# The first tokens' projections with their features in two quarters and one half, in a fused transformer block on one Trainium2 core

## The chip, the cores and the metric

The kernel runs on one core of a Trainium2 chip. The metric is the device time of one execution in microseconds (us). Each run's time is listed; a profile is one further execution with the hardware profiler on. Engines are named as in the profile: PE (TensorE matmul), PEld (its weight load), DVE (VectorE), ACT (ScalarE), POOL (GpSimd), SP (SyncE, which here issues nearly all DMA transfers).

## What is computed

One adaptive-layernorm transformer block over 2048 tokens of 1024 features, in float32. A vector c gives six modulation vectors, two of which (`sa`, `ca`) shift and scale the normalized input of the attention:

```python
mod = (_silu(L0_c) @ L0_wmod).reshape(L0_c.shape[0], 6, 1, -1)
sa, ca, ga, sb, cb, gb = (mod[:, 0], mod[:, 1], mod[:, 2], mod[:, 3], mod[:, 4], mod[:, 5])
...
h = _layernorm(x, axis=-1) * (1 + ca) + sa
x = x + ga * _L0_attn_ref(h, L0_attn_Wq, L0_attn_Wk, L0_attn_Wv, L0_attn_Wo)
h = _layernorm(x, axis=-1) * (1 + cb) + sb
x = x + gb * _L0_ffn_ref(h, L0_ffn_route_w, L0_ffn_A, L0_ffn_Bw)
```

The attention has 32 query heads and 8 key and value heads of 32 features, rotary positions and a causal mask. The feed-forward part routes each token to one of 8 low-rank experts. What matters here is the very first stage: `q = h @ Wq`, `k = h @ Wk`, `v = h @ Wv` for the first 256 tokens, where h needs `ca` and `sa`.

## The kernel before

The features (1024) lie in 8 chunks of 128 on the partitions. `h_t` holds h transposed: [128, 8 chunks, 256 tokens].

**Modulation** (L846 to L907). `Modulation(i, half)` makes 512 of the 1024 features of modulation vector i. It has two parts. The first, `mr` (L874), multiplies the matrix wmod, which comes in four w tiles of [128, 2, 512] (256 rows and 512 columns each, 512 KB), by the vector silu(c), and copies the result to `rows` on DVE (L880). The second, `mc` (L886), turns the rows into columns, one per chunk, and writes them to `mod_cols[i]` on DVE (L892 or L894). i = 1 is the scale `ca` (plus one), i = 0 the shift `sa`.

**Project** (L940). `Project(b)` handles 256 tokens in two token tiles of 128: `flip` transposes the normalized x on PE into a PSUM bank (L835) and applies scale and shift on the way to `h_t`, on ACT for the first half of the features (L822) and on DVE for the second (L826). Then values and keys (L764, `by_columns`) and queries (L1059) accumulate over the chunks. `keep_values` copies the values on ACT; `keep_keys` and `keep_queries` apply the rotary positions on DVE and POOL (L933 to L938).

**Streams** (L659). `weights` is a queue of loads with a pool of NW = 5 tiles, `tokens` one with NX = 4. `pump` issues the next loads while a buffer is free, `free(n)` gives n buffers back and pumps. Loads are issued in order on SP, and a load into a buffer waits on SP until PE has read the buffer's earlier tile. Eight DMA semaphores are used in turn, so that a load also waits for the one eight places before it.

**The opening** (`open_up`, L1507) is an order written out by hand. `fill(n)` issues the next n parts of the items; the first four items are Modulation (1, half 0), (0, half 0), (1, half 1), (0, half 1). The opening issues both parts of the first two, then the flips of the features 0 to 511 (`kh` = 0), then values, keys and queries over these four chunks, with the third and fourth Modulation between them, then the flips and the projections of the features 512 to 1023. The weights of the first two projections stay resident: `vk` tiles hold four chunks of wv and wk side by side, `wq` tiles two chunks of half of wq's columns. In the middle stand the loads of the second half, of the rotary tables cos and sin (`load_rotation`) and of the next tokens; near the end the norm of the second project's x (`second.pre()`). Six PSUM banks hold the sums of values, keys and four query groups; the two others are used in turn by Modulation and flips.

After the opening a planner (`plan_order`, with estimated costs of each part) sets the order of everything that is left. That order is fixed when the kernel is built.

Of the kernel before, what the change touches and what calls it, by code (L numbers as in the profile page):

```python
# [11 lines left out]
F32 = mybir.dt.float32  # L12
# [6 lines left out]
P = 128  # L19
T = 2048  # L20
D = 1024
# [5 lines left out]
QB = 512  # L27
NQB = T // QB
TB = 256
# [523 lines left out]
def adaln_block_kernel(  # L553
# [24 lines left out]
    nc = tc.nc  # L578
# [15 lines left out]
    ident = const.tile([P, P], F32, name="ident")  # L594
# [64 lines left out]
    class Stream:  # L659
        def __init__(self, pool, tag, depth):  # L660
            self.pool, self.tag, self.depth = pool, tag, depth
            self.loads, self.tiles = [], []
            self.freed = self.used = 0

        def pump(self, most=1 << 30):
            while len(self.tiles) < min(len(self.loads), self.freed + self.depth, most):
                n = len(self.tiles)
                shape, load = self.loads[n]
                t = self.pool.tile(shape, F32, tag=self.tag, name=f"{self.tag}_{n}")
                load(t)  # L670
                self.tiles.append(t)
# [14 lines left out]
    weights = Stream(wpool, "w", NW)  # L686
    tokens = Stream(xpool, "x", NX)

    def want_wmod(i, half):
        for kp in range(NC // 2):  # L690
            col = i * D + half * 512
            src = wmod[kp * 2 * P : (kp + 1) * 2 * P, col : col + 512].rearrange(
                "(k p) n -> p k n", p=P
            )
            weights.loads.append(([P, 2, 512], lambda t, s=src: nc.sync.dma_start(t, s)))

    resident = {}

    def load_values_keys(kh):

        rows = slice(kh * 512, (kh + 1) * 512)
        t = epool.tile([P, 4, QB], F32, tag="et", name=f"vk_{kh}")
        for i, w in enumerate((wv, wk)):
            nc.sync.dma_start(
                t[:, :, i * TB : (i + 1) * TB], w[rows, :].rearrange("(k p) n -> p k n", p=P)
            )
        resident["vk", kh] = t

    def load_queries(kh, half):
        for kp in (2 * kh, 2 * kh + 1):  # L710
            t = qpool.tile([P, 2, QB], F32, tag="q", name=f"wq_{half}_{kp}")
            nc.sync.dma_start(
                t,
                wq[kp * 2 * P : (kp + 1) * 2 * P, half * 512 : (half + 1) * 512].rearrange(
                    "(k p) n -> p k n", p=P
                ),
            )
            resident["q", half, kp] = t

    def want_qkv():  # L720
        for w in (wv, wk):
# [124 lines left out]
    class Modulation:  # L846
# [1 line left out]

        when = -1

        def __init__(self, i, half):
            self.i, self.half = i, half

        def plan(self, push):
            slow = 0.2 if self.i in mod_cols else 2.4
            return [
                Part(1.7, "C", True, (("dve", 0.7),), chunks=4, push=push),
                Part(0.9, "W", True, (("dve", slow),), frees=4),
            ]

        def want(self):
            want_wmod(self.i, self.half)

        def pre(self):
            return []

        def main(self, following):
            i, half = self.i, self.half
            parts = weights.take(4)
            ps = bank(f"mr_{i}_{half}")  # L870
            for r in range(2):
                for q in range(4):
                    k = r * 4 + q
                    nc.tensor.matmul(  # L874
                        ps[q * HD : (q + 1) * HD, :], silu_p[:, k, :], parts[k // 2][:, k % 2, :],
                        start=(r == 0), stop=(r == 1),
                    )
                weights.free(2)
            rows = two.tile([P, 512], F32, tag="half", bufs=3, name=f"rows_{i}_{half}")
            nc.vector.tensor_copy(rows, ps)  # L880
            following()
            yield 1.7, True
            ps = bank(f"mc_{i}_{half}")
            if i in mod_cols:
                for j in range(4):
                    nc.tensor.matmul(  # L886
                        ps[:, j : j + 1], rows[:, j * P : (j + 1) * P], ones_p[:, 0:1],
                        start=True, stop=True,
                    )
                dst = mod_cols[i][:, half * 4 : half * 4 + 4]  # L890
                if i in (1, 4):
                    nc.vector.tensor_scalar_add(dst, ps[:, 0:4], 1.0)  # L892
                else:
                    nc.vector.tensor_copy(dst, ps[:, 0:4])  # L894
            else:


                nc.tensor.matmul(ps, ones_p, rows, start=True, stop=True)
                cols = slice(half * 512, (half + 1) * 512)
                sgn = two.tile([P, 512], F32, tag="half", bufs=3, name=f"gsgn_{i}_{half}")  # L900
# [39 lines left out]
    class Project:  # L940
# [521 lines left out]
    m = {(i, half): Modulation(i, half) for i in (2, 3, 4, 5) for half in range(2)}  # L1462
# [35 lines left out]
    def fill(n=1):  # L1498
        for _ in range(n + 4):
            step = advance()  # L1500
            assert step is not None
            n -= bool(step[0])
            if not n:
                return step[0]
        raise AssertionError("the next part of an item cannot be issued yet")

    def open_up():  # L1507


# [6 lines left out]
        load_values_keys(0)  # L1516
        load_queries(0, 0)
        fill(2)
        opening.start()
        for s in range(2):  # L1520
            opening.flip(s, 0)
        chosen[:0] = range(6)
        banks = [bank("open") for i in range(6)]

        def values(kh):
            for s in range(2):
                for k in range(4 * kh, 4 * kh + 4):
                    opening.value(banks[0], s, k)

        def keys(kh):  # L1530
            for a in range(2):
                for k in range(4 * kh, 4 * kh + 4):
                    opening.key(banks[1], a, k)

        def queries(kh, i):
            for a in range(2):
                for k in range(4 * kh, 4 * kh + 4):
                    opening.query(banks[2 + i], i // 2, 2 * (i % 2) + a, k)

        values(0)  # L1540
        keys(0)
        load_queries(0, 1)
        fill(2)
        load_values_keys(1)
        for half in range(2):
            load_queries(1, half)
        tokens.pump()
        cs = load_rotation(0, 2)
        for i in range(4):
            opening.query_tiles(i // 2, i % 2)  # L1550
        queries(0, 0)
        queries(0, 1)
        fill(2)
        queries(0, 2)
        for s in range(2):
            opening.flip(s, 1)
            tokens.free()
        sign_rotation(cs)
        for _, act in second.pre():
            act()  # L1560
        queries(0, 3)
        values(1)
        keys(1)
        opening.keep_values(banks[0])
        opening.keep_keys(banks[1])
        for half in range(2):
            for hp in range(2):
                queries(1, 2 * half + hp)
            for hp in range(2):
                opening.keep_queries(banks[2 + 2 * half + hp], half, hp)  # L1570
        chosen.clear()
# [357 lines left out]
```

## Time and profile before

| | us |
|---|---|
| time, median of 3 runs | 1755.12 (1754.39 to 1757.01) |
| the profiled execution's own time | 1754.72 |
| its span | 1753.0 |
| mean granted clock of the span | 0.996 |

The first 60 us, in windows of 10 us (busy time of each engine in us; PEclk is the granted clock of PE, 1.00 is full speed):

| from:to us | PE | DVE | ACT | POOL | PEclk | GB/s moved |
|---|---|---|---|---|---|---|
| 0:10 | 1.20 | 1.19 | 2.77 | 8.73 | 1.00 | 263 |
| 10:20 | 8.47 | 5.12 | 3.19 | 0.00 | 0.83 | 361 |
| 20:30 | 9.13 | 0.85 | 2.90 | 0.00 | 1.00 | 384 |
| 30:40 | 9.16 | 0.85 | 0.00 | 0.00 | 1.00 | 366 |
| 40:50 | 9.16 | 2.25 | 0.00 | 0.00 | 1.00 | 386 |
| 50:60 | 10.00 | 6.32 | 4.26 | 0.00 | 1.00 | 372 |

In this stage the transfers run all the time, and PE is the busiest engine from 10 us on. A matmul's busy time is modelled, so that PE can count as busy while it waits a little between two matmuls.

### The profile page before, as it was taken

To read this page: it belongs to the slowest core of one execution; us is meant where nothing else is said; L and a number is where in the kernel's file an instruction comes from. 1 tells how busy PE (TensorE), PEld (TensorE's weight loads), DVE (VectorE), ACT (ScalarE), POOL (GpSimd) and SP (SyncE) were. 2 spreads that over 40 slices of the span, in tenths; PEclk is the share of its full clock that TensorE was granted. 3 is DMA by queue.
4 is the path that set the end of the run, shared out by engine and by line. 5 is a ranking of instruction groups with operands and counts; after the bars stand their busy time and mean duration, and the time that the engine had idled before them with its cause. 6 is when DMAs were issued, how large, how long until landed. Compare 5 with 4: busy or idle time off the path is not lost.

```text
span 1753.0 us, 55172 instructions
## 1 busy us (share of the span) xinstructions
PE 1716.7 (98%) x24616; PEld 700.3 (40%) x24616; DVE 1084.6 (62%) x2140; ACT 740.4 (42%) x1643; POOL 1296.5 (74%) x640
## 2 busy tenths in 40 slices
PE   7999999999999999999999999999999999999998
PEld 3655554444444433334444443323323333333333
DVE  1455556756656764675667545756675675776486
ACT  2203423443543433445435444244444544454463
POOL 1235646478878775869786989789889899898951
PEclk9999999999999999999999999999999999999999
DMA  9502323212322512222013011110111111101001
GB/s 346 193 27 80 115 84 104 63 62 98 104 63 66 180 72 83 73 79 67 24 60 128 26 50 49 68 44 37 50 54 46 48 50 50 73 26 49 34 5 50
DMA packets 69069, 130.52 MB, mean 74 GB/s; under 512 B 3808, under 2 KB 20832, under 8 KB 68832
## 3 DMA queue, kind: packets, MB, share of 16 engines
q1 hardware_dynamic: 67504, 125.85, 20.9%
q8 instruction: 193, 3.16, 0.8%
q10 hardware_dynamic: 1328, 1.15, 0.2%
q14 instruction: 44, 0.36, 0.1%
HBM read 118.59 MB, written 8.39 MB: 72 GB/s over the span
## 4 chain that ended last, share of the span: by engine, by line
PE 77%; POOL 14%; DVE 3%; issue 2%; DMA 1%; ACT 1%; POOLq 0%; SPq 0%; DVEq 0%; ACTq 0%
PE sm L1618 13%; POOL acc L1744 12%; PE po L1726 11%; PE sc L1708 11%; PE pq L1059 11%; PE pw L764 10%; PE sc L1694 4%; PE pk L764 3%; PE pv L764 2%; PE pd L1753 2%; PE open L1059 2%; DVE mx L1625 1%; PE pf L764 1%; PE pa L764 1%; PE sm L1605 1%
## 5 line engine op out<-in xcount | busy, mean ns | idle before, releaser
L1625 DVE TENSOR_REDUCE mx<-sm 128x1 f32<-128x512 f32 (+3 forms) x1280 | 687.4, 604 | 400.1 <-PE sm L1618 399.2
L1744 POOL TENSOR_TENSOR acc<-acc,et 128x2048 f32<-128x2048 f32 (+1 forms) x242 | 905.0, 3739 | 27.6 <-ACT et L1716 14.2
L1716 ACT ACTIVATE et<-sc 128x512 f32<-128x512 f32 (+3 forms) x1280 | 575.5, 545 | 662.0 <-PE sc L1708 646.1
L1618 PE MATMUL sm<-k_t,q 32*128 32x512 f32 (+3 forms) x3328 | 335.5, 474 | 3.1 <-ACT rd L1760 3.0
L1726 PE MATMUL po<-et,v_sb 128*32 128x512 f32 (+3 forms) x2560 | 296.0, 538 | 0.6 <-ACT et L1716 0.5
L1708 PE MATMUL sc<-q,k_t 32*128 32x512 f32 (+3 forms) x2560 | 290.9, 533 | 0.0
L764 PE MATMUL pw<-w,q 128*32 128x512 f32 x1920 | 235.4, 597 | 1.4 <-DMA w<-in_wo_dram 1.4
L1618 PEld LDWEIGHTS sm<-k_t,q 32*128 32x128 f32 x3328 | 139.1, 185 | 131.4 <-issue 48.8
L1059 PE MATMUL pq<-h_t,w 128*32 128x256 f32 x3072 | 187.9, 382 | 0.0
L1742 POOL TENSOR_TENSOR acc<-et,et 128x2048 f32<-128x2048 f32 (+1 forms) x31 | 132.1, 4262 | 38.5 <-ACT et L1716 24.8
L1059 PEld LDWEIGHTS pq<-h_t,w 128*32 128x32 f32 x3072 | 90.5, 109 | 103.9 <-issue 48.8
L1205 POOL TENSOR_TENSOR x<-ag,x 128x512 f32<-128x512 f32 x40 | 64.3, 1609 | 90.2 <-DVE ag L1204 81.5
L1726 PEld LDWEIGHTS po<-et,v_sb 128*32 128x32 f32 x2560 | 61.5, 108 | 166.3 <-issue 137.1
L1708 PEld LDWEIGHTS sc<-q,k_t 32*128 32x128 f32 x2560 | 118.9, 184 | 14.1 <-issue 2.8
L1764 DVE RECIPROCAL rd<-rd 128x128 f32<-128x128 f32 x124 | 110.0, 925 | 13.8 <-ACT rd L1760 13.6
L1694 PE MATMUL sc<-nt,ones_h 32*128 32x512 bf16 (+3 forms) x1280 | 115.1, 351 | 1.8 <-DVE mx L1625 1.0
L1694 PEld LDWEIGHTS <-ones_h 32*128 32x128 bf16 x1280 | 31.1, 91 | 196.8 <-issue 187.0
L764 PEld LDWEIGHTS pw<-w,q 128*32 128x32 f32 x1920 | 51.3, 109 | 139.5 <-issue 117.0
L937 POOL TENSOR_TENSOR swap_q<-swap_q,cs 128x512 f32<-128x512 f32 x32 | 40.8, 1275 | 60.9 <-DVE swap_q L934 60.8
L937 POOL TENSOR_TENSOR swap_k<-swap_k,cs 128x512 f32<-128x512 f32 x8 | 10.2, 1276 | 95.3 <-DVE swap_k L934 95.3
L1204 DVE TENSOR_TENSOR ag<-pw,gate 128x512 f32<-128x512 f32 x40 | 27.5, 688 | 63.3 <-PE pw L764 61.4
L1768 POOL TENSOR_TENSOR q<-q,rd 128x512 f32<-128x512 f32 x31 | 39.5, 1274 | 35.5 <-DVE rd L1764 28.8
(166 smaller groups left out, 1275.9 us busy)
## 6 DMA issues: line engine op xcount, KB each, us to landing
w<-in_wo_dram SPq DMA_DIRECT2D x112, 256.0 KB
w<-in_wmod_dram SPq DMA_DIRECT2D x48, 512.0 KB
w<-in_wq_dram SPq DMA_DIRECT2D x48, 512.0 KB
x<-in_x_dram SPq DMA_DIRECT2D x32, 512.0 KB
w<-in_wv_dram SPq DMA_DIRECT2D x12, 512.0 KB
w<-in_wk_dram SPq DMA_DIRECT2D x12, 512.0 KB
out_dram<-x SPq DMA_DIRECT2D x12, 512.0 KB
wq<-in_wq_dram SPq DMA_DIRECT2D x8, 512.0 KB
```

What stands on the lines that cost most here:

```text
L764: nc.tensor.matmul(dst[rows], left[:, rows], right, start=start, stop=stop)
L1059: nc.tensor.matmul(ps[j * HD : (j + 1) * HD, a * TB : (a + 1) * TB], self.query_weights(half, k, j * P + h * HD), self.h_t[:, k, :], start ...
L1205: nc.gpsimd.tensor_add(x1[t][:, cols], tmp, x1[t][:, cols])
L1618: nc.tensor.matmul(ps[j][:, a:b], q[rows, t * P : (t + 1) * P], k[rows, kc * QB + o : kc * QB + o + b - a], start=not masked, stop=(t, a, ...
L1625: nc.vector.tensor_reduce(mx[:, t, j : j + 1, kc], ps[j][:, a:b], AX.X, ALU.max)
L1694: nc.tensor.matmul(ps[j][:, a:b], ones_h[rows, :], nt[rows, off:], start=(kc == kcs[0]), stop=False,)
L1708: nc.tensor.matmul(ps[j][:, a:b], k[rows, kc * P : (kc + 1) * P], q[rows, off:], start=False, stop=(kc == kcs[-1]),)
L1716: nc.scalar.activation(self.ets[kc][:, j, off:], ps[j][:, a:b], AF.Exp, scale=1.0 / math.sqrt(HD))
L1726: nc.tensor.matmul(self.po[rows, off:], v_sb[:, kc, 4 * (self.m // 4) + j, :], et[:, j, off:], start=(i == 0), stop=(i == self.nk - 1),)
L1742: self.adder.tensor_add(self.acc[:, :, off:], first[:, :, off:], et[:, :, off:])
L1744: self.adder.tensor_add(self.acc[:, :, off:], self.acc[:, :, off:], et[:, :, off:])
L1764: nc.vector.reciprocal(part, part)
```

## The change

The first two Modulation items are now made of two pieces each: the first has 256 features of scale and the same 256 of shift, the second the next 256 of both. The third and fourth have 512 features of scale and of shift, as before. A tile of the first two is loaded by two DMAs of 256 columns. `Stream` remembers a limit `most` that holds back later loads. The loads of wv, wk and wq for the opening come in steps of two chunks (256 features). The opening projects the features 0 to 255 (values, keys, all four query groups), then 256 to 511, then 512 to 1023; a new `flip_chunks` transposes two chunks of both token tiles into one bank and applies scale and shift on ACT, 256 columns at a time. Between the two parts of a Modulation item half a query group is issued.

```diff
-        def pump(self, most=1 << 30):
-            while len(self.tiles) < min(len(self.loads), self.freed + self.depth, most):
+            self.most = 1 << 30
+
+        def pump(self, most=None):
+            self.most = most or self.most
+            while len(self.tiles) < min(len(self.loads), self.freed + self.depth, self.most):
...
+            def load(t, kp=kp):
+                at = 0
+                for i, col, n in pieces:
+                    nc.sync.dma_start(
+                        t[:, :, at : at + n],
+                        wmod[kp * 2 * P : (kp + 1) * 2 * P, i * D + col : i * D + col + n].rearrange(
+                            "(k p) n -> p k n", p=P
+                        ),
+                    )
+                    at += n
...
-                dst = mod_cols[i][:, half * 4 : half * 4 + 4]
-                if i in (1, 4):
-                    nc.vector.tensor_scalar_add(dst, ps[:, 0:4], 1.0)
-                else:
-                    nc.vector.tensor_copy(dst, ps[:, 0:4])
+                at = 0
+                for i, col, n in self.pieces:
+                    dst, n = mod_cols[i][:, col // P : (col + n) // P], n // P
+                    if i in (1, 4):
+                        nc.vector.tensor_scalar_add(dst, ps[:, at : at + n], 1.0)
+                    else:
+                        nc.vector.tensor_copy(dst, ps[:, at : at + n])
+                    at += n
...
+        def flip_chunks(self, k0):
+
+            ps = bank(f"tr_a_{self.b}_{k0}")
+            for i in range(2):
+                for s in range(2):
+                    nc.tensor.transpose(
+                        ps[:, (2 * i + s) * P : (2 * i + s + 1) * P],
+                        self.xt[s][:, (k0 + i) * P : (k0 + i + 1) * P], ident,
+                    )
+            for i in range(2):
+                modulate(
+                    self.h_t[:, k0 + i, :], ps[:, i * TB : (i + 1) * TB],
+                    mod_cols[1], mod_cols[0], k0 + i, True,
+                )
...
-    start_items = [Modulation(i, half) for half in range(2) for i in (1, 0)]
+    start_items = [Modulation((1, col, TB), (0, col, TB)) for col in (0, TB)]
+    start_items += [Modulation((i, 512, 512)) for i in (1, 0)]
...
         tokens.pump(2)
-        weights.pump()
+        weights.pump(4)
+        load_values_keys(0)
+        for half in range(2):
+            load_queries(0, half)
+        weights.most = 8
         chosen.extend([6, 7] * 8)
         for _, act in opening.pre():
             act()
         fill(2)
...
+        load_values_keys(1)
+        for half in range(2):
+            load_queries(1, half)
+        opening.start()
+        opening.flip_chunks(0)
...
+        values_keys([0])
+        for i in range(3):
+            queries([0], i)
+        queries([0], 3, [0])
+        weights.most = 12
+        fill(1)
+        load_values_keys(2)
+        load_values_keys(3)
+        queries([0], 3, [1])
+        fill(1)
+        opening.flip_chunks(2)
+
+        values_keys([1])
+        queries([1], 0)
+        queries([1], 1)
+        weights.most = 1 << 30
+        fill(1)
+        for half in range(2):
+            for kp in (2, 3):
+                load_queries(kp, half)
+        cs = load_rotation(0, 2)
+        tokens.pump(1 << 30)
+        queries([1], 2, [0])
+        fill(1)
+        queries([1], 2, [1])
+        queries([1], 3, [0])
+        fill(1)
+        queries([1], 3, [1])
+        fill(1)
+        for k in (4, 6):
+            opening.flip_chunks(k)
+        tokens.free(2)
         sign_rotation(cs)
         for _, act in second.pre():
             act()
-        queries(0, 3)
-        values(1)
-        keys(1)
+
+        values_keys([2, 3])
         opening.keep_values(banks[0])
         opening.keep_keys(banks[1])
         for half in range(2):
             for hp in range(2):
-                queries(1, 2 * half + hp)
+                queries([2, 3], 2 * half + hp)
```

More of the change, by code (lines that the diff above doesn't have):

```diff
@@ L687, in adaln_block_kernel, with want_wmod @@
     tokens = Stream(xpool, "x", NX)
-    def want_wmod(i, half):
+    def want_wmod(pieces):
         for kp in range(NC // 2):
[L691 to L695, printed above, removed]
-    resident = {}
-    def load_values_keys(kh):
-        rows = slice(kh * 512, (kh + 1) * 512)
-        t = epool.tile([P, 4, QB], F32, tag="et", name=f"vk_{kh}")
+            def load(t, kp=kp):
[8 more added lines that the diff above has]
+                    at += n
+            weights.loads.append(([P, 2, 512], load))
@@ L703, in load_values_keys @@
+    resident = {}
+    def load_values_keys(kp):
+        rows = slice(kp * 2 * P, (kp + 1) * 2 * P)
+        kh, at = kp // 2, kp % 2 * 2
+        if kp % 2 == 0:
+            resident["vk", kh] = epool.tile([P, 4, QB], F32, tag="et", name=f"vk_{kh}")
         for i, w in enumerate((wv, wk)):
             nc.sync.dma_start(
-                t[:, :, i * TB : (i + 1) * TB], w[rows, :].rearrange("(k p) n -> p k n", p=P)
-            )
[L707 to L718, printed above, removed]
+                resident["vk", kh][:, at : at + 2, i * TB : (i + 1) * TB],
+                w[rows, :].rearrange("(k p) n -> p k n", p=P),
+            )
@@ L720, in want_qkv, with load_queries @@
+    def load_queries(kp, half):
+        t = qpool.tile([P, 2, QB], F32, tag="q", name=f"wq_{half}_{kp}")
+        nc.sync.dma_start(
+            t,
+            wq[kp * 2 * P : (kp + 1) * 2 * P, half * 512 : (half + 1) * 512].rearrange(
+                "(k p) n -> p k n", p=P
+            ),
+        )
+        resident["q", half, kp] = t
     def want_qkv():
@@ L849, in adaln_block_kernel, with __init__ @@
         when = -1
-        def __init__(self, i, half):
-            self.i, self.half = i, half
+        def __init__(self, *pieces):
+            self.pieces = pieces
         def plan(self, push):
-            slow = 0.2 if self.i in mod_cols else 2.4
+            slow = 0.2 if self.pieces[0][0] in mod_cols else 2.4
             return [
@@ L861, in want @@
         def want(self):
-            want_wmod(self.i, self.half)
+            want_wmod(self.pieces)
         def pre(self):
@@ L867, in main @@
         def main(self, following):
-            i, half = self.i, self.half
+            i, col, _ = self.pieces[0]
             parts = weights.take(4)
-            ps = bank(f"mr_{i}_{half}")
+            ps = bank(f"mr_{i}_{col}")
             for r in range(2):
@@ L878, in main @@
                 weights.free(2)
-            rows = two.tile([P, 512], F32, tag="half", bufs=3, name=f"rows_{i}_{half}")
+            rows = two.tile([P, 512], F32, tag="half", bufs=3, name=f"rows_{i}_{col}")
             nc.vector.tensor_copy(rows, ps)
@@ L882, in main @@
             yield 1.7, True
-            ps = bank(f"mc_{i}_{half}")
+            ps = bank(f"mc_{i}_{col}")
             if i in mod_cols:
@@ L889, in main @@
                     )
-                dst = mod_cols[i][:, half * 4 : half * 4 + 4]
-                if i in (1, 4):
-                    nc.vector.tensor_scalar_add(dst, ps[:, 0:4], 1.0)
-                else:
-                    nc.vector.tensor_copy(dst, ps[:, 0:4])
+                at = 0
[6 more added lines that the diff above has]
+                    at += n
             else:
                 nc.tensor.matmul(ps, ones_p, rows, start=True, stop=True)
-                cols = slice(half * 512, (half + 1) * 512)
-                sgn = two.tile([P, 512], F32, tag="half", bufs=3, name=f"gsgn_{i}_{half}")
+                cols = slice(col, col + 512)
+                sgn = two.tile([P, 512], F32, tag="half", bufs=3, name=f"gsgn_{i}_{col}")
                 nc.vector.tensor_scalar(sgn, ps, 0.0, 0.5, ALU.is_ge, ALU.subtract)
@@ L1025, in flip @@
             )
+        def flip_chunks(self, k0):
[10 more added lines that the diff above has]
+                    mod_cols[1], mod_cols[0], k0 + i, True,
+                )
         def first(self, part, k):
@@ L1459, in adaln_block_kernel @@
     opening, second = Project(0), Project(1)
-    start_items = [Modulation(i, half) for half in range(2) for i in (1, 0)]
+    start_items = [Modulation((1, col, TB), (0, col, TB)) for col in (0, TB)]
+    start_items += [Modulation((i, 512, 512)) for i in (1, 0)]
     early, late = outputs(0)
-    m = {(i, half): Modulation(i, half) for i in (2, 3, 4, 5) for half in range(2)}
+    m = {(i, half): Modulation((i, half * 512, 512)) for i in (2, 3, 4, 5) for half in range(2)}
     phases = [
@@ L1515, in open_up @@
         fill(2)
[L1516 to L1543, printed above, removed]
         load_values_keys(1)
@@ L1546, in open_up, with queries, values_keys @@
             load_queries(1, half)
-        tokens.pump()
-        cs = load_rotation(0, 2)
+        opening.start()
+        opening.flip_chunks(0)
+        chosen[:0] = range(6)
+        banks = [bank("open") for i in range(6)]
         for i in range(4):
             opening.query_tiles(i // 2, i % 2)
[L1551 to L1557, printed above, removed]
+        def queries(kps, i, parts=range(2)):
+            for a in parts:
+                for k in range(2 * kps[0], 2 * kps[-1] + 2):
+                    opening.query(banks[2 + i], i // 2, 2 * (i % 2) + a, k)
+        def values_keys(kps):
+            for s in range(2):
+                for k in range(2 * kps[0], 2 * kps[-1] + 2):
+                    opening.value(banks[0], s, k)
+            for a in range(2):
+                for k in range(2 * kps[0], 2 * kps[-1] + 2):
+                    opening.key(banks[1], a, k)
+        values_keys([0])
[29 more added lines that the diff above has]
+        tokens.free(2)
         sign_rotation(cs)
```

## The prediction

> **What bounds the kernel now.** The page's first and fourth parts come first: how busy each engine is, and which engine holds the chain of work that ended last.
>
> ```profile
> PE 1716.7 (98%) x24616; PEld 700.3 (40%) x24616; DVE 1084.6 (62%) x2140; ACT 740.4 (42%) x1643; POOL 1296.5 (74%) x640
> ...
> PE 77%; POOL 14%; DVE 3%; issue 2%; DMA 1%; ACT 1%; POOLq 0%; SPq 0%; DVEq 0%; ACTq 0%
> ```
>
> TensorE (PE) is busy for 1716.7 of 1753.0 us, so 36.3 us are idle. Later work stands in a fixed order behind PE, so the opening matters as PE's idle time and as the moment when its last matmul (L1059, open<-h_t,wq) ends. The order of the two built kernels, with names stripped of numbers, is the same on every engine from there on. So I read the chain of waits from 8 to 75 us (start, length, what).
>
> ```profile
> 15.45 1.25 PE mc L886 x8
> 16.70 3.44 PE mr L874 x16
> ...
> 20.16 0.70 DVE rows L880
> ...
> 20.91 1.05 PE mc L886 x8
> 21.96 0.51 PE tr_a L835 x4
> ...
> 22.50 0.47 ACT h_t L822
> ...
> 23.01 7.11 PE open L764 x128
> 30.12 1.79 PE mr L874 x16
> ...
> 31.93 0.70 DVE rows L880
> ...
> 59.49 13.81 PE open L1059 x256
> ```
>
> From 15.45 us on PE works nearly without a gap until 59.49 + 13.81 = 73.30 us. Its waits there are few: a slow second mr, three times the copy "rows" on VectorE (DVE), once the first h_t on ScalarE (ACT). All that the change can win after 15.45 us is in these waits. Before 15.45 us the chain is x, rot_sb and DVE's norm steps, ending in the first rows at 14.70 us. The first item's matmuls are over by 8.80 + 5.12 = 13.92 us, so that start has 0.8 us of slack.
>
> **The change part by part.** I call the Modulation items M0 to M3; each has matmuls mr, the copy rows, and matmuls mc.
>
> Removed from PE's path:
> 1. The second mr took 3.44 us, against 1.79 in the later ones. It now stands behind the first quarter's projections. Price: 3.44 - 1.79 = 1.65 us.
> 2. Three rows waits: 20.14 to 20.91, 31.91 to 32.68, 42.56 to 43.33, each 0.77 us: 2.31. In the new order half a query group stands between mr and mc: 32 of the matmul records of which 128 took 7.04 us, so 0.88 to 0.90 us. That covers 0.77. Without the cover each returns 0.77.
> 3. The wait for the first h_t, 22.47 to 23.01: 0.54 us.
> 4. The first values and keys take 7.11 us, the later ones 6.91: 0.20 us of waiting for ACT's eight h_t pieces.
>
> Sum removed: 4.70 us.
>
> Added:
> 5. Each of the first two quarters is flipped (transposes, then two ACT pieces 128x256) straight before its values. The nearest rows are h_t 128x128 at 473 ns, and for the exponential 128x256 at 390 against 128x128 at 313 ns. So one piece takes 473 + 77 = 550 ns, and with the pipeline's 0.02 and 0.04 around it the wait is 0.6 us: twice, 1.2 us. Its second piece is hidden: one feature chunk of values for one token tile is 0.43 us of PE (6.91 / 16). The last half needs two banks of transposes; the second bank's 0.51 us covers the first ACT piece, so about zero. If VectorE's two mod copies (0.16 us each) came after the transposes they would add up to 0.3 us; they run under them. Bounds for the two waits: 0.9 to 2.0 us.
> 6. The first chain shows only 4 of the first 8 transposes, the other 4 ran inside the wait of point 3. Now all 16 stand on the path: +0.51 us.
> 7. Loads. The stream holds five w tiles, so tile n+5 is issued when tile n is read, and SP is in order. Up to M2 everything lands early. By the sum of PE pieces M1's mr runs at about 28 us, M2's at 40, M3's at 45.6. The tiles of M3 other than the first wait for M2's reads: tiles 13 and 14 issue at about 41, tile 15 at 42. Queued behind them on SP are one wv tile, the four last wq loads, cos, sin and two x tiles; these are needed at 57 us or later and land by 58 us at 1.36 us per 512 KB. A transfer into an empty queue costs 1.6 us (c_sb: 0.79 to 2.39 in the chain) plus 1.36 us per 512 KB (the weight loads below resume at 10.17, 11.53 and 12.87 us, each at a landing). So 13, 14 and 15 land at 44, 45.3 and 46.7 us; the last is read 0.9 us after mr begins, at 46.5: +0.25 us, between 0 and 1.6 (the 1.6 if they land as slowly as the kernel's first three loads).
>
> ```profile
> 10.17 0.19 PEld L874 LDWEIGHTS mr<-w,silu_p 128*32 128x32 f32 x4 [1.19 <-DMA w<-in_wmod_dram]
> 11.53 0.19 PEld L874 LDWEIGHTS mr<-w,silu_p 128*32 128x32 f32 x4 [1.18 <-DMA w<-in_wmod_dram]
> 12.87 0.14 PEld L874 LDWEIGHTS mr<-w,silu_p 128*32 128x32 f32 x4 [1.15 <-DMA w<-in_wmod_dram]
> ```
>
> 8. Eight wmod tiles come as two loads of 256 columns, rows of 1 KB in place of 2 KB: eight more issues on SP at about 0.45 us, hidden because SP runs ahead of the transfers. While wv and wk landed with 1 KB rows the transfers ran at 372 GB/s, against 386 GB/s with 2 KB rows, so M0's four tiles are some 0.2 to 0.5 us later. The 0.8 us of slack before the first rows hides that: 0. The old loads of vk in one piece become two, at no cost to PE.
> 9. The PE clock. Three windows of 3.4 us, with PE's busy time second and PEclk (granted clock) near the end:
>
> ```profile
> 12.68:16.10 3.42, 1.89 (x12) 0.83 (x11) 2.38 (x11) 2.64 (x4) 0.00 (x0) 1.00 0.99 341
> 16.10:19.50 3.40, 3.40 (x18) 1.26 (x19) 0.16 (x1) 0.14 (x1) 0.00 (x0) 0.50 1.01 349
> 19.51:22.92 3.41, 2.61 (x22) 1.73 (x16) 0.85 (x2) 0.42 (x2) 0.00 (x0) 1.00 1.08 375
> ```
>
> After a window in which PE was busy 1.89 of 3.42 us the clock was halved for one window; after 2.61 of 3.41 it was not. Before, the halved window fell on the second mr, and its cost is inside point 1. Now the same idle time (13.92 to 15.45) is followed by four transposes and the first values: transposes +0.5 us, then from 18.3 to 19.5 values at half speed, +0.6: 1.1 us. The Trainium skill ("TensorE: Matmul & The Clock Gate", Part 1) says that the clock drops only after at least one idle window of about 3.4 us, and that windows run freely. By that rule 1.5 us of idle time costs nothing and the sum is 1.1 us better. The row shows the drop after 1.5 us, so I take the row, and keep the rule's value for the range.
>
> Sum added: 1.2 + 0.51 + 0.25 + 1.1 = 3.06 us. Net 4.70 - 3.06 = 1.6 us gained; the last opening matmul should end at about 71.7 us. Against its own execution: 1754.72 - 1.6 = 1753.1; that execution is 0.4 below the median 1755.12, so for a median **1753.5 us**.
>
> Behind the opening the x tiles of the second project arrive some 5 us later than before (about 57 us), so DVE reaches the key's rotary at about 61 instead of 59.6; it has caught up before the second project, whose transposes need x only at 71.7.
>
> **Rivals.**
> - A, the clock windows fall well: their phase is free, so the halved window may miss the opening (1.1 us), and the stall near 294 to 297 us, behind which PEclk is 0.50 from 296 to 300 us and 0.65 from 300 to 304 (two windows), may cost one window, saving half of 3.4 = 1.7. 1753.5 - 2.8 = 1750.7. For it: the two halves are seen in the trace. Against: the same stalls are still there.
> - B, the M3 loads take the place of the removed waits: SP stands still twice (M1's and M2's reads), the queue drains, and tile 15 lands 2.3 us later than in point 7; PE idles then over 2 of 3.4 us, and the clock is halved for one window, 1.7. 1753.5 + 4.0 = 1757.5. It is slower than before from the point where tile 15 lands about 1 us late and the clock drops. For it: before, the transfers ran without a break to 62 us. Against: it needs a landing twice as slow as c_sb and the spacing give.
> - C, the change doesn't do what it says: the first values read a tile vk that also gets the second quarter's wv and wk. If they waited for those (the queue's 14th 512 KB; the 6th landed at 12.87 us, eight more at 1.36 to 1.45 us make about 24.2) instead of 18.3, +6 us: 1759.5. In the built order the first values wait on another semaphore than that load's, so this is unlikely.
>
> **How the numbers follow.** Forecast 0.50; A 0.28, and some 0.02 for more; B 0.16; C 0.04. The forecast's own range is 1751.7 to 1755.5 (point 5 +-0.6, point 7 up to 1.35, point 9 1.1 either way). The range to 8 in 10 reaches to A and B: 1749.8 to 1758.0. Within 0.2% (3.5 us, about what a measurement can tell from no change) is the forecast with part of A and B: 0.52. Faster by more: most of A, 0.30. Slower: the worse half of B, C and what I haven't seen, 0.18.
>
> **What would show it.** mr once early, then tr_a and open at about 18.3 us; PE's idle "rows" waits gone after the first; two waits on ACT h_t near 18 and 32.5 us of 0.6; at M3 a wait on DMA w under 0.5 us; the last L1059 open ending near 71.7 us and the transposes of the second project right behind it; PEclk at half only near 16 to 19.5 us. It is wrong if first values begin after 20 us, if M3 waits for more than 1 us, or if the opening's gain is not there at the end.

## The result, and the profile after

The changed kernel is slower: 1757.21 us median (22 runs, 1754.92 to 1759.35) against 1754.42 us for the original on the same chip (22 runs, 1752.94 to 1757.01). The ratio is 1.0017, 95% interval 1.0011 to 1.0023, so 1.9 to 4.0 us. The forecast was 1.6 us the other way. The profiled execution of the changed kernel took 1756.68 us, its span is 1755.0 us, its mean granted clock 0.997.

The page's first and fourth parts, of the changed kernel:

```profile
PE 1717.1 (98%) x24616; PEld 699.4 (40%) x24616; DVE 1081.3 (62%) x2134; ACT 741.6 (42%) x1643; POOL 1296.4 (74%) x640
...
PE 72%; POOL 18%; DVE 3%; issue 3%; DMA 3%; ACT 1%; POOLq 0%; SPq 0%; DVEq 0%; ACTq 0%
```

PE's busy time is what it was (1716.7 before), and the span grew by 2.0 us: these are waits. In the chain, PE lost five points of share, POOL gained four and DMA two. These shares don't show where: three of POOL's four points are the attention's `acc` (12% before, L1744; 15% after, L1792), far behind the opening. The place is read from the timelines.

PE's timeline from the end of the opening on, first of the original (start, length, line, what, number of instructions, and in brackets the idle time before them and what ended it; the last row of each such list is cut at the end of the window that was read):

```profile
73.24 1.97 PE L835 MATMUL tr_a<-ident,x 128*128 128x128 f32 x16
75.14 7.11 PE L764 MATMUL pv<-vk,h_t 128*32 128x256 f32 x128
82.07 4.28 PE L764 MATMUL pk<-h_t,vk 128*32 128x256 f32 x76
```

The same of the changed kernel, with the opening's waits ahead:

```profile
17.05 1.96 PE L776 MATMUL open<-vk,h_t 128*32 128x256 f32 x32 [0.66 <-ACT h_t L834]
...
31.53 1.96 PE L776 MATMUL open<-vk,h_t 128*32 128x256 f32 x32 [0.66 <-ACT h_t L834]
...
46.28 0.62 PE L886 MATMUL mr<-w,silu_p 128*32 128x512 f32 x2 [0.29 <-DMA w<-in_wmod_dram]
...
71.26 1.97 PE L847 MATMUL tr_a<-ident,x 128*128 128x128 f32 x16
74.33 1.93 PE L776 MATMUL pv<-vk,h_t 128*32 128x256 f32 x32 [1.11 <-DVE swap_q L949]
78.00 5.39 PE L776 MATMUL pv<-vk,h_t 128*32 128x256 f32 x96 [1.73 <-DVE h_t L838]
83.21 2.99 PE L776 MATMUL pk<-h_t,vk 128*32 128x256 f32 x52
```

The opening did what it was meant to: the second project's transposes begin 1.98 us earlier (71.26 against 73.24), though a part of this is the clock, which was halved for a while in the original's opening and not in this one (point 9 below). But its keys, pk, begin 1.14 us later (83.21 against 82.07). In twelve microseconds 3.1 us are lost, in two waits of 1.11 and 1.73 us on DVE that the original does not have, and in the values broken up by them. By the profile the first wait ends with a shuffle (`swap_q`) and the second with `h_t`. DVE's timeline, of the original:

```profile
59.56 0.69 DVE L933 TENSOR_TENSOR tcos_k<-open,cs 128x512 f32<-128x512 f32 x1 [3.33 <-DMA x<-in_x_dram]
...
67.35 0.01 DVE L934 LOAD_MASK_SELECT swap_q<-open  x1 [0.19 <-POOL q L938]
...
70.85 0.01 DVE L934 LOAD_MASK_SELECT swap_q<-open  x1 [0.24 <-POOL q L938]
...
74.35 0.01 DVE L934 LOAD_MASK_SELECT swap_q<-open  x1 [0.28 <-POOL q L938]
74.35 0.74 DVE L934 STREAM_SHUFFLE swap_q<-open 128x512 f32<-128x512 f32 x1
74.98 2.63 DVE L826 TENSOR_SCALAR h_t<-tr_a,mod,mod 128x128 f32<-128x128 f32 x8
```

and of the changed kernel:

```profile
57.13 1.28 DVE L786 BATCH_NORM_STATS2 stats_a<-x 128x6 f32<-128x512 f32 x2 [7.75 <-DMA x<-in_x_dram]
...
62.12 0.68 DVE L948 TENSOR_TENSOR tcos_k<-open,cs 128x512 f32<-128x512 f32 x1
...
66.41 0.01 DVE L949 LOAD_MASK_SELECT swap_q<-open  x1 [2.37 <-POOL k_t L953]
...
76.94 0.72 DVE L949 STREAM_SHUFFLE swap_q<-open 128x512 f32<-128x512 f32 x1
77.56 2.63 DVE L838 TENSOR_SCALAR h_t<-tr_a,mod,mod 128x128 f32<-128x128 f32 x8
```

DVE waits 7.75 us for the next tokens' x, then does their norm (57.13 to 62.1), and only then begins the rotary positions of the opening's keys, tcos_k, although PE had finished these keys at 57.33. From there the five rotaries follow each other: the shuffle of the keys at 62.73, those of the four query groups at 66.41, 69.92, 73.47 and 76.94, every 3.5 us. They do not catch up: tcos_k is 2.56 us later than in the original (62.12 against 59.56), and the second half of the second project's h_t, which stands behind the last shuffle on DVE, is 2.58 us later (77.56 against 74.98). What sets the 3.5 us is in the changed kernel's chain of waits (start, length, what):

```profile
63.73 1.29 POOL swap_k L952
...
65.09 1.29 POOL k_t L953
...
66.41 0.76 DVE swap_q L949 x2
```

A rotary is a shuffle on DVE (0.75 us), a product on POOL (1.29) and a sum on POOL (1.29), with small gaps between them. Its two temporaries come from a pool of three buffers (tag "half"), so that the next shuffle waits until POOL's sum has given them back. This is a loop of 3.5 us, and PE makes a query group in 3.45 us (13.81 / 4): the loop has no slack, and a late start stays late to the end. In the original's rows the shuffle's wait for POOL already grows from group to group, 0.19, 0.24, 0.28 us.

### The profile page after: what moved, and what is told of

Same layout as the page of the kernel before. It is cut to its first block, busy times and chain, and to the rows that moved or that the text cites. A ratio compares the mean times of both kernels' runs of the same rounds, so it can differ in the third digit from the quotient of the medians.

```text
span 1755.0 us, 55194 instructions
## 1 busy us (share of the span) xinstructions
PE 1717.1 (98%) x24616; PEld 699.4 (40%) x24616; DVE 1081.3 (62%) x2134; ACT 741.6 (42%) x1643; POOL 1296.4 (74%) x640
## 4 chain that ended last, share of the span: by engine, by line
PE 72%; POOL 18%; DVE 3%; issue 3%; DMA 3%; ACT 1%; POOLq 0%; SPq 0%; DVEq 0%; ACTq 0%
POOL acc L1792 15%; PE sm L1666 13%; PE pq L1089 11%; PE po L1774 11%; PE sc L1756 10%; PE pw L776 9%; PE sc L1742 4%; PE pk L776 3%; PE pv L776 2%; PE pd L1801 2%; DVE mx L1673 1%; PE pf L776 1%; PE sm L1653 1%; PE pa L776 1%; DMA w<-in_wmod_dram 1%
## 5 line engine op out<-in xcount | busy, mean ns | idle before, releaser
L1792 POOL TENSOR_TENSOR acc<-acc,et 128x2048 f32<-128x2048 f32 (+1 forms) x242 | 905.0, 3740 | 28.3 <-ACT et L1764 15.0
```

The source lines that it names most:

```text
L1792: self.adder.tensor_add(self.acc[:, :, off:], self.acc[:, :, off:], et[:, :, off:])
```

## The experiments

Theory T: the opening's gain is real and is lost because x arrives late, so that DVE's norm stands in front of a rotary loop that cannot catch up. Rivals: the loss lies in the opening or in the 256-column loads themselves (R1); it is the clock, halved more often (R2); it is the order of all that follows, changed timing against a fixed order (R3). Every kernel was timed beside the original on the same chip; ratios are to the original, with the 95% interval. The matmuls called busy in three of them are extra and read by nobody.

**x_first.** The changed kernel, with the loads of x and of the rotary tables put ahead of the four last wq loads on SP.

```diff
+        tokens.pump(1 << 30)
+        cs = load_rotation(0, 2)
         for half in range(2):
             for kp in (2, 3):
                 load_queries(kp, half)
-        cs = load_rotation(0, 2)
-        tokens.pump(1 << 30)
```

> The changed kernel, but the two x tiles of the second project and the rotary tables are issued ahead of the last four wq loads. Nothing else moves. Theory (the norm of the late x holds VectorE, so that the key's rotary starts at 62.1 us instead of 57.5, and the rotary chain of 3.5 us a group cannot make it up while PE makes a group in 3.45 us): x lands about 5 us earlier, the first tcos_k starts at 57.5 us, the second project's values begin at 72.5 to 73 us without the waits of 1.11 and 1.73 us, and the key matmuls pk begin some 2 us before the original's 82.07. Time about 1752.5, 2 below the original (ratio 0.9985 to 0.9995). Rival 1 (the stall comes from something else in the new order of the opening, such as the banks or the second project's weights): waits and time as in the changed kernel, ratio 1.0017. Rival 2 (the later phases lose by themselves): the waits go, but the time stays above the original's.

Measured: 1753.00 us, 0.9991 [0.9985, 0.9998]. Moving four DMA issues removes the loss, and both waits on DVE are gone. R1 and R3 fall: the quarters, their loads and the order of all later work are as in the changed kernel. Whether it is a gain over the original this ratio alone does not show, since a copy of the original reads 0.9993 below; the table by clock does. Its profile had a halved window in the opening, and pk begins at 82.39, not the expected 2 us before the original's 82.07; x_first_busy below, at full clock, has that.

**x_middle.** The same loads ahead of only two of the four.

```diff
-        for half in range(2):
-            for kp in (2, 3):
-                load_queries(kp, half)
-        cs = load_rotation(0, 2)
+        for kp in (2, 3):
+            load_queries(kp, 0)
         tokens.pump(1 << 30)
+        cs = load_rotation(0, 2)
+        for kp in (2, 3):
+            load_queries(kp, 1)
```

> The changed kernel, with the x tiles and the rotary tables ahead of two of the four last wq loads instead of behind all four (x_first: ahead of all). Theory: x lands 2.7 us earlier than in the changed kernel, tcos_k starts at 59 to 60 us instead of 62.1, some 2 us late; the time lies between x_first and the changed kernel, ratio 0.9995 to 1.0008. Rival (only whether x comes before the queries' weights matters, by which load is late for PE): equal to one of the two, 0.9991 or 1.0017.

Measured: 1753.97 us, 0.9998 [0.9991, 1.0004], between the two, but its interval overlaps that of x_first, so a dose is not shown. In its profile tcos_k begins at 60.53, 1.37 us after PE had the keys (59.16), and PE has neither wait (pk at 81.91): that much lateness the second project bears. In the changed kernel it is 62.12 - 57.33 = 4.79 us.

**norm_later.** The changed kernel with x as late as it is, but with its norm put on DVE behind the first two query groups' rotaries.

```diff
-        for _, act in second.pre():
-            act()
...
             for hp in range(2):
                 opening.keep_queries(banks[2 + 2 * half + hp], half, hp)
+            if half == 0:
+                for _, act in second.pre():
+                    act()
```

> The changed kernel with its late x, but the second project's norm stands behind the rotaries of the first two query groups in the program, so that VectorE turns keys and two query groups first. Loads as in the changed kernel. Theory: tcos_k starts at 57.5 us and the chain keeps pace with PE; the norm runs at about 66 to 71 us, so the second project's transposes wait for x until about 71.5 to 72.5 us, and the waits on DVE behind them are under 1.5 us; time 1 to 2.5 us below the changed kernel, ratio 1.0000 to 1.0010. Rival (late loads, not VectorE's order): no change, ratio 1.0017.

Measured: 1753.64 us, 0.9997 [0.9989, 1.0006]. DVE's timeline of norm_later:

```profile
57.66 0.69 DVE L948 TENSOR_TENSOR tcos_k<-open,cs 128x512 f32<-128x512 f32 x1 [8.21 <-PE open L776]
...
66.09 1.27 DVE L786 BATCH_NORM_STATS2 stats_a<-x 128x6 f32<-128x512 f32 x2
```

tcos_k now starts as soon as PE has the keys, and PE's waits shrink to 0.22 us (for the normalized x) and 0.55 us (for h_t). The late x does its harm through DVE's order.

**own_swaps.** The changed kernel, x late and the norm in front, but the four query rotaries get shuffle buffers of their own, so that the loop is open.

```diff
-        swap = two.tile([P, 2, TB], F32, tag="half", name=f"swap_{name}", bufs=3)
+        if spare:
+            swap = spare.pop(0).rearrange("p (a n) -> p a n", a=2)
+        else:
+            swap = two.tile([P, 2, TB], F32, tag="half", name=f"swap_{name}", bufs=3)
```

> The changed kernel with its late x, but the four query rotaries of the opening get a swap buffer each, so that VectorE's shuffle of a group no longer waits for GpSimd's add of the group before. Theory (late start and a chain that cannot catch up are both needed): tcos_k still starts at 62.1 us, but the shuffles then follow within some 2 us of PE, the last one at about 72 instead of 76.94, and the two waits of PE in the second project (2.84 us) go or fall under 1 us; time about 2 to 3 us below the changed kernel, ratio about 1.000. Rival (the late start alone matters, or the buffers don't): the last shuffle stays at about 77 us, ratio 1.0017.

Measured: 1753.67 us, 0.9995 [0.9987, 1.0003]. DVE's timeline of own_swaps:

```profile
63.92 0.68 DVE L952 TENSOR_TENSOR tcos_k<-open,cs 128x512 f32<-128x512 f32 x1
...
73.81 0.74 DVE L953 STREAM_SHUFFLE swaps<-open 128x512 f32<-128x512 f32 x1
74.45 2.64 DVE L838 TENSOR_SCALAR h_t<-tr_a,mod,mod 128x128 f32<-128x128 f32 x8
```

tcos_k is even later than in the changed kernel (63.92 against 62.12), yet the last shuffle is 3.1 us earlier (73.81 against 76.94), and PE does not wait. This profile had a halved window; against the changed kernel's second profile, which had one too (changed_again below: tcos_k at 64.11, last shuffle at 78.93), it is 5.1 us earlier. POOL's products now follow each other every 2.60 us (68.12, 70.73, 73.33, 75.92). The lateness harms only because the loop has no slack.

**before_x_late.** The original with its tables and x put behind the Modulation item that follows, and so behind the weight loads that this item's reads set free.

```diff
-        tokens.pump()
-        cs = load_rotation(0, 2)
...
         fill(2)
+        cs = load_rotation(0, 2)
+        tokens.pump()
```

> The original kernel with its halves, in which only the loads of the rotary tables and of the second project's x are moved behind four later weight loads (2 MB, some 5.5 us). Theory: x lands at about 56 to 57 us, tcos_k starts at 61 to 62 instead of 59.56 us, the last shuffle some 2 us later than 74.35, and the second project's values wait 1 to 2.5 us for VectorE; time 1 to 2.5 us above the original, ratio 1.0006 to 1.0015, without any of the change. Rival (the quarters themselves cost the time): ratio 1.0000.

Measured: 1755.89 us, 1.0008 [0.9999, 1.0016]. PE's timeline of before_x_late:

```profile
72.86 1.97 PE L835 MATMUL tr_a<-ident,x 128*128 128x128 f32 x16
...
77.82 5.39 PE L764 MATMUL pv<-vk,h_t 128*32 128x256 f32 x96 [1.13 <-DVE h_t L826]
83.02 3.21 PE L764 MATMUL pk<-h_t,vk 128*32 128x256 f32 x56
```

The same wait appears without any quarters. The interval just reaches 1, so the ratio alone would not show it; at the same granted clock the medians are 0.9 to 1.5 us above the original's (table below).

**The clock, R2.** In some profiles PE's granted clock was halved for 3.4 us in the opening, in others not, for the same kernel. Two kernels keep PE occupied there with eight matmuls: after the first mr of M0 and after the first transposes.

```diff
-        fill(2)
+        fill(1)
+        busy("busy_1", 384)
+        fill(1)
...
+        busy("busy_2", 256)
```

x_first_busy is x_first with them, changed_busy the changed kernel.

> x_first, with eight matmuls more whose sums nobody reads: four of 384 columns between the first mr and its mc, four of 256 columns behind the first transposes. They keep PE busy in its two idle stretches near 14.0 to 14.9 and 16.4 to 17.0 us. Theory (whether PE's clock is halved for one 3.4 us window in the opening depends on how the windows fall over these idle stretches, and costs the new order some 2 us: x_first's profiled execution was halved from 16.9 to 20.3 us and its opening ended at 73.6 instead of 71.3 us): the clock is never halved in the opening, the second project's transposes begin at about 71.4 us in every execution, and the median is 0.5 to 1.2 us below x_first's 1753.0, ratio to the original about 0.9985. Rival (the clock follows something else, or the extra matmuls delay mc and the values by as much): median at or above x_first's, ratio 0.9991 or more.

> The changed kernel with the same eight extra matmuls, x as late as in the changed kernel. Theory (the second project waits for VectorE's rotary chain, which starts when the late x has been normed, so that what PE gains in the opening is given back): although the opening always ends at about 71.4 us, pk begins at 83 us as before and the time is that of the changed kernel, ratio 1.0013 to 1.0019. Rival (the changed kernel loses by its halved clock): ratio about 1.000 or below.

Measured: x_first_busy 1752.44 us, 0.9984 [0.9976, 0.9991], its slowest run 1753.20 (x_first's was 1755.94); changed_busy 1756.34 us, 1.0006 [0.9998, 1.0015], below the band that was expected. Neither profile has a halved window in the opening. The ratio of changed_busy lies between theory and rival, so by itself it leaves the clock a part of the loss. x_first_busy is the best version: faster than both kernels of this case.

The record settles R2 further, for each run has the mean granted clock of its span, to three digits. A window of 3.41 us at half speed lowers it by 0.001 (half of 3.41 in 1753). Median times in us at the same clock, their number in brackets (three runs at 0.994 and 0.995 are left out; the 22 runs of the original in the first section have no clock on record):

| kernel | 0.996 | 0.997 | 0.998 |
|---|---|---|---|
| original, in three groups | 1756.16 (36) | 1754.56 (56) | 1753.16 (35) |
| original_again | 1756.02 (1) | 1754.23 (8) | 1752.79 (4) |
| changed and changed_again | 1758.62 (13) | 1756.99 (19) | 1754.95 (6) |
| before_x_late | 1757.10 (2) | 1755.88 (8) | 1754.61 (2) |
| norm_later | 1755.97 (2) | 1754.80 (4) | 1752.67 (6) |
| own_swaps | 1755.08 (3) | 1753.53 (10) | none |
| x_first | 1754.80 (7) | 1752.96 (9) | 1751.23 (5) |
| x_first_busy | none | 1752.79 (8) | 1751.63 (7) |

At the same clock the changed kernel takes 1.8 to 2.5 us more than the original, and x_first 1.4 to 1.9 us less, where a copy of the original strays by 0.1 to 0.4. The mean over all runs is 0.9968 for the changed kernel and 0.9970 for the original, which is some 0.3 us (an estimate from these two means). So how often the clock is halved is not the main cause of the loss.

PE's timeline of x_first_busy:

```profile
71.26 1.97 PE L847 MATMUL tr_a<-ident,x 128*128 128x128 f32 x16
73.16 7.11 PE L776 MATMUL pv<-vk,h_t 128*32 128x256 f32 x128
80.09 6.23 PE L776 MATMUL pk<-h_t,vk 128*32 128x256 f32 x112
```

The transposes begin at 71.26 as in the changed kernel's profile, and pk 3.12 us earlier than there.

**original_busy** is the original with sixteen such matmuls, eight in each of the first two rows waits (`fill(2)` becomes `fill(1)`, `busy`, `fill(1)`, as above); **original_again** is a copy of the original, **changed_again** a copy of the changed kernel.

> The original, with sixteen unread matmuls of 256 columns: eight between the first mr and its mc, eight between the second mr and its mc, where PE waits for the copy rows. It tells how much of x_first_busy's 0.9984 is the quarters and how much the steadier clock. Theory (quarters): the original's halved window in the opening costs it only some 0.4 to 1 us, so this one is within 0.0006 of the original, ratio 0.9994 to 1.0000, and x_first_busy stays 1.5 us or more below it. Rival (the clock alone): ratio 0.9985, as x_first_busy.

> The original once more, as another kernel, for the size of differences that mean nothing and for a second profile: ratio 1.0000 with an interval of some 0.0007 to each side; the second project's transposes at 72.9 us if the clock isn't halved in the opening, at 73.2 us if it is.

> The changed kernel once more, for a second profile beside the other kernels' runs. Theory: ratio 1.0010 to 1.0020. If its clock is halved in the opening, M1's and M2's mr are some 2 us later, and since the w loads that stand ahead of x on SP wait for them, x lands and tcos_k starts later too (64 us, as in own_swaps' halved profile); if not, tcos_k starts at 62.1 us. Rival (x's landing doesn't depend on PE's pace): 62.1 us in both cases.

Measured: original_busy 1754.40 us, 0.9999 [0.9991, 1.0007], so busy matmuls alone are no gain that can be seen; original_again 1754.13 us, 0.9993 [0.9985, 1.0001], which is how far a copy can stray (its transposes came at 73.68 with a halved window, where 73.2 was expected); changed_again 1757.03 us, 1.0016 [1.0008, 1.0024]: the loss repeats. Its profile had the halved window that the first profile of the changed kernel lacked. PE's timeline of changed_again:

```profile
17.31 3.39 PE L776 MATMUL open<-vk,h_t 128*32 128x256 f32 x32 [0.66 <-ACT h_t L834]
...
48.79 0.62 PE L886 MATMUL mr<-w,silu_p 128*32 128x512 f32 x2 [1.20 <-DMA w<-in_wmod_dram]
...
80.00 5.39 PE L776 MATMUL pv<-vk,h_t 128*32 128x256 f32 x96 [1.74 <-DVE h_t L838]
85.20 1.05 PE L776 MATMUL pk<-h_t,vk 128*32 128x256 f32 x16
```

The first 32 value matmuls take 3.39 us instead of 1.96; M3's last tile is waited for 1.20 us instead of 0.29; and tcos_k comes at 64.11 instead of 62.12. In SP's timeline the load of x is issued at 48.77 instead of 46.25: it stands behind the w tiles, whose buffers PE must have read. So pk is another 2 us later. changed_busy has no halving in its profile, which fits its coming out better than expected.

All twelve profiles together, in us; the last column is the execution's own time less the start of pk:

| kernel | clock halved in the opening | second project's transposes | pk begins | time after |
|---|---|---|---|---|
| original | yes | 73.24 | 82.07 | 1672.65 |
| original_again | yes | 73.68 | 82.51 | 1671.53 |
| original_busy | no | 72.37 | 81.20 | 1673.55 |
| before_x_late | no | 72.86 | 83.02 | 1672.97 |
| changed | no | 71.26 | 83.21 | 1673.47 |
| changed_again | yes | 73.77 | 85.20 | 1673.04 |
| changed_busy | no | 71.12 | 82.75 | 1671.60 |
| norm_later | no | 71.62 | 81.47 | 1671.23 |
| own_swaps | yes | 73.00 | 81.83 | 1673.19 |
| x_middle | yes | 73.09 | 81.91 | 1673.06 |
| x_first | yes | 73.57 | 82.39 | 1672.41 |
| x_first_busy | no | 71.26 | 80.09 | 1672.73 |

What follows pk takes 1671.2 to 1673.6 us whatever the kernel, and this spread is mostly the clock again: in the three profiles below 1671.7 the clock's record has one halved window near 300 us, in the nine others (1672.4 to 1673.6) two in a row. So the difference is made before 85 us. The start of pk is read like with like: the changed kernel has it at 83.21 at full clock, against 81.20 in original_busy, and at 85.20 with a halved window, against 82.07 and 82.51 in the original: 2.0 us later, and 2.7 to 3.1. The runs say 1.9 to 4.0. How often the halved window falls in the opening, beyond these profiles (four of the six with quarters and no busy matmuls), was not counted.

## Why the prediction was wrong

**The step that failed** is its last sentence before the rivals: DVE reaches the key's rotary "at about 61 instead of 59.6; it has caught up before the second project". The lateness was seen, and nearly sized (x was put at 57 us and came at 57.1; 61 became 62.1). What was assumed without a row is the catching up. The rows were there before the change: query shuffles at 63.84, 67.35, 70.85 and 74.35 in the original's DVE timeline, the last three waiting for POOL's sum of the one before, every 3.5 us beside PE's 3.45 us a query group. A loop that does not outpace PE returns no delay. Put at nothing, this step cost 3.12 us: from the second project's transposes to pk it is 11.95 us in the changed kernel (71.26 to 83.21) and 8.83 in x_first_busy (71.26 to 80.09). x_first, norm_later and own_swaps each cut one link of that chain (late load, order on DVE, shared buffers), and each brings the time back to about the original's or below. With the late load mended, x_first gains what the sum had forecast: 1.59 us (1753.00 against 1754.59 of the original beside it) beside 1.6. That the two agree so well is luck in part, for the terms below were off in both directions.

**Points 1 to 4, removed**: right. Rows waits after the first are gone, the second mr takes 1.72 us in the chain, and the first values start at 17.05 us, before the 18.3 that was put with a halved clock.

**Point 5**: two waits on ACT of 0.66 us, forecast 0.6. The third flip showed 0.22 us, forecast about zero; the first value groups took 3.68 us instead of 3.46, twice. Together some 0.8 us more than the sum held (0.12 + 0.22 + 0.44). **Point 6**: transposes 0.51 us, as put.

**Point 7**: the wait on M3's last tile was 0.29 us, forecast 0.25, and the tile was there at 46.28, forecast 46.7. In the four profiles with quarters and full clock it is 0.29 to 0.35 us, in the four with a halved window 0.55 to 1.20 (changed_again, beyond the 1 us that was named as a sign of being wrong). Rival B's drained queue is real in both of the changed kernel's profiles, but costs little. Windows of 4 us from the start of M2's mr on, first of the original (busy us of PE, PEld, DVE, ACT, POOL; then granted clock, share of DMA time, GB/s):

```profile
40.00:44.00 4.00, 3.16 (x38) 1.40 (x31) 0.69 (x1) 0.00 (x0) 0.00 (x0) 1.00 1.08 372
```

of the changed kernel, where that mr starts at 38.49:

```profile
38.30:42.30 4.00, 4.00 (x52) 2.08 (x48) 0.69 (x1) 0.00 (x0) 0.00 (x0) 1.00 0.49 144
```

and of changed_again, where it starts at 40.19:

```profile
40.00:44.00 4.00, 4.00 (x52) 2.07 (x48) 0.69 (x1) 0.00 (x0) 0.00 (x0) 1.00 0.56 151
```

**Point 8**: put at nothing because of 0.8 us of slack, and this slack belonged to one profile. In the changed kernel the first rows began when mr ended (14.01, 14.03), so nothing hid a late tile. The first mc begins at 14.87, before the 15.45 of the original's profile; but in the three other profiles of the original's order it begins at 14.63 to 14.67. Against these M0's tiles cost 0.2 us, and 0.5 in changed_again (15.14).

**Point 9, the clock**: mis-sized in both directions. In the profile of the changed kernel it cost nothing. Where it fell, in changed_again, it halved 16.89 to 20.31 us. By the second mr that execution is 1.71 us behind (28.30 against 26.59), 0.27 of it from before the halved window (mc at 15.14 against 14.87), and by the second project's transposes 2.51 (73.77 against 71.26); the sum had 1.1. The last 0.8 us are the longer wait for M3's last tile. It was issued as long after M2's mr as in the changed kernel's first profile (2.46 and 2.45 us) and landed later; why stays open. The forecast end of the opening, 71.7 us, lies between the two and was met by neither. Like with like the quarters gain 1.1 to 1.7 us of opening at full clock (71.12 and 71.26 against 72.37 and 72.86), and nothing when halved (73.0 to 73.8 against 73.24 and 73.68).

**The rivals**: the first half of A, a full clock in the opening, was seen in one profile and did not save the time, since pk was late all the same; the two halved windows near 300 us were still there. B's drained queue was there, but its wait was 0.29 and 1.20 us, not the main loss. C did not happen: the first values waited for ACT alone and began at 17.05 us. No rival named the rotary loop, and a slower result was given 0.18.

## What to carry to other kernels

When a change delays a load, follow the instruction that waits for it down its own in-order queue, and ask of each loop behind it not whether it is fast but whether it is faster than the engine it serves: a loop of 3.5 us beside a cadence of 3.45 us hands every delay on. An edit that makes the front of a kernel start earlier has to bring the next stage's loads forward too; here the order of eight DMA issues (four moved past four) decided the sign. And where a change is worth less than executions differ, compare the start of one late instruction in several profiles, and times at the same granted clock.

## What the runs showed of the hardware

PE's clock was halved after windows in which PE was mostly busy, and whether it was depends on a phase that differs between executions of the same program. The trace's record of the clock begins at 11.41 us in the changed kernel and at 13.48 in changed_again, each time with full speed. Ahead of that the views print 1.00 because nothing is recorded; the first row of the table of windows before the change has its 1.00 from there. The matmuls themselves were slow: the first item's mr of the changed kernel (ns of one, shortest, median and longest, then start of the first and the last), and the second item's:

```profile
L886 PE MATMUL mr<-w,silu_p x16: 589/760/1061, 8.4 to 13.4; 128*32 128x512 f32 x16
L886 PE MATMUL mr<-w,silu_p x16: 592/592/592, 26.6 to 27.9; 128*32 128x512 f32 x16
```

From there on the record has steps of 3.41 us. The first two such windows of the changed kernel, columns as above:

```profile
11.41:14.82 3.41, 2.13 (x10) 0.34 (x8) 2.36 (x10) 2.77 (x4) 0.00 (x0) 1.00 1.09 366
14.82:18.24 3.42, 2.71 (x36) 1.95 (x40) 0.23 (x2) 1.03 (x3) 0.00 (x0) 1.00 1.08 361
```

and of changed_again, the same program:

```profile
13.48:16.89 3.41, 2.30 (x16) 1.31 (x12) 0.92 (x3) 1.27 (x2) 0.00 (x0) 1.00 1.06 376
16.89:20.31 3.42, 3.00 (x30) 1.37 (x34) 0.00 (x0) 0.83 (x2) 0.00 (x0) 0.50 1.11 349
```

PE was busy 2.30 us before the halved window and 2.13 before the one that was not halved. No amount of busy time separates the two: over the profiles of the opening the halved windows follow 1.89 to 2.55 us of busy time, and windows with 2.02, 2.13, 2.16 and 2.62 were followed by full speed. (A busy time holds waits inside a group of matmuls, so it is not PE's work.) The phase does separate them in the six profiles with quarters and no busy matmuls: where the record begins at 11.41 or 11.47 us nothing is halved, where it begins at 13.25 to 13.50 one window is. The Trainium skill ("TensorE: Matmul & The Clock Gate", Part 1) says that the clock falls after at least one idle window of some 3.4 us and that windows run freely. Between the start of the record and the halved window of the opening no profile has an idle window of that length; the longest idle stretches that PE's timeline of changed_again shows between 10 and 17.5 us are 0.88 and 0.66 us; here the measurement decides against the first part. The record agrees with the second: its steps lie at 11.41 us in one execution and at 13.48 in another of the same program.

Eight matmuls of no use in those gaps went with full clock in both profiles that had them after the change. Since the record begins at 12.22 and 12.28 us there, a phase that no profile with quarters and without them had, this does not show that they prevented a halving. The runs say more: of the 41 runs of the three kernels with busy matmuls one has a mean clock of 0.996 or less, of the 187 of the original, the changed kernel and x_first 57.
